# Embedding of patch tokens: four neighbours from five products instead of two from three

## The chip, the cores and the metric

One core of one Trainium2 chip runs the whole kernel. The metric is device time in microseconds (us), the median of three runs. Engines are called PE (TensorE, matmul), DVE (VectorE), ACT (ScalarE), POOL (GpSimd) and SP (SyncE, which here only issues transfers). SBUF is the working memory, 128 partitions wide; PSUM is where matmuls leave their results.

## What is computed

The reference cuts a signal into overlapping patches, takes a real Fourier transform of each, and embeds it with one matrix. What follows is one attention-like layer with a decaying memory and a mixture of eight experts, two of them for each token.

```python
# tokenizer: x is (4, 64, 512, 64) = (B, C, T, V); patches of 16 with stride 8, last value repeated 8 times
patches = xp[:, :, idx, :]                      # idx = n * 8 + 0..15, n = 0..63
xf = rfft(patches, axis=patch, norm='ortho')    # 9 frequencies
h = concat([xf.real, xf.imag]) @ W.T            # W is 256 x 1152: 16384 tokens of 256

# layer
z  = layernorm(layernorm(h))
q, k, v = z @ Wq.T + bq, z @ Wk.T + bk, z @ Wv.T + bv
mem[t] = decay * mem[t-1] + k[t] * v[t];  z1 = ln(h) + q * mem
h  = h + z1 + relu(layernorm(z1) @ W1.T + b1) @ W2.T + b2

# experts: the two best of eight for each token
tok = layernorm(h)
h  = h + tok + sum over the two experts e of weight_e * (gelu(tok @ w1[e] + b1[e]) @ w2[e] + b2[e])
```

Transform and W are linear, so they fold into one matrix over the 16 samples of a patch and the 64 channels. A patch is two halves of 8 samples, and neighbouring patches share a half. If s(n) is the n-th segment of 8 samples, token n is s(n) A + s(n+1) B, which is a short convolution along n.

## The kernel before

The tokens go through in 32 blocks of 512, four tiles of 128 each. A pair of samples shares a partition group, so a product with A or B is four matmuls of 128 x 128 by 128 x 256, summed in PSUM (J = 4). The folded weights are kept as E and O, the even and the odd frequencies, with A = E + O and B = E - O. Two neighbours come from three products: one of the odd segment with 2E, which both share, and one of each difference.

```python
weff = emb.tile([P, 2 * J, D], F32)          # E + O, E - O
wsum = emb.tile([P, J, D], F32)              # 2 E
xpool: bufs=2                                # xb, the segments of one block

def differences(self, xb):
    self.xd = emb.tile([P, 2, J, NV, NO], F32, name="xd")
    nc.vector.tensor_tensor(self.xd[:, 0], ev[:, :, :, :NO], od, ALU.subtract)     # L305
    nc.vector.tensor_tensor(self.xd[:, 1], ev[:, :, :, 1:], od, ALU.subtract)      # L306

def embed(self):
    ps = p_tm.tile([P, U, D], F32, name="tm")
    for u in range(U):                       # U = 2
        for j in range(J):
            nc.tensor.matmul(ps[:, u, :], lhsT=od[:, j, ts(u, P)], rhs=wsum[:, j, :], ...)   # L317
    ms = emb.tile([P, U, D], F32, name="ms")
    nc.scalar.copy(ms, ps)                   # L321
    for u in range(U):
        yield                                # other work of PE comes in between
        ps = p_tm.tile([P, 2, D], F32, name="tm")
        for i in range(2):
            for j in range(J):
                nc.tensor.matmul(ps[:, i, :], lhsT=xd[:, i, j, ts(u, P)], rhs=weff[:, i * J + j, :], ...)  # L328
        nc.vector.tensor_tensor(self.h[:, u::U, :], ps, ms[:, u:u+1, :].to_broadcast([P, 2, D]), ALU.add)  # L335
        for i in range(2):
            norm.stats(self.h, i * U + u)    # bn_stats, bn_aggr
    norm.factors(twice=True)                 # rstd, on GpSimd
    norm.apply(self.zz, self.h, 1)
    norm.apply(self.z, self.h, 0)
```

What follows in a block, with the buffers that matter. `zz` and `tok` are turned into features by a transposing DMA through 16-bit halves; `turned` has one buffer, and the join reads it.

```python
class Turn:
    def start(self, planes):                                     # L272
        self.turned = one.tile([P, TT, 2, KD, P], U16, name="turned")
        ... nc.sync.dma_start(out=turned part, in_=plane, transpose=True)
    def join(self, dst, copy):                                   # L278: hT and tokT
        ...

def retention(self, m):                                          # m = 0, 1
    pk = feature_mm(wqkv_sb[:, 1], self.hT, m)                   # L284, bank mm of four
    nc.scalar.activation(own_order(ks), tiles_order(pk), AF.Identity, bias=...)
    pv = feature_mm(wqkv_sb[:, 2], self.hT, m)
    nc.vector.scalar_tensor_tensor(kv, tiles_order(pv), bv, ks, ALU.add, ALU.mult)      # L374
    nc.vector.tensor_tensor_scan(ks, decay, kv, carry, ALU.mult, ALU.add)               # L382
    pq = feature_mm(wqkv_sb[:, 0], self.hT, m)
    nc.vector.scalar_tensor_tensor(tiles_order(ret), tiles_order(pq), bq, ks, ALU.add, ALU.mult)   # L392
```

The order of PE, DVE, ACT and SP is written by hand. One turn of the loop works on three blocks (`new`, `mid`, `old`); `slot` takes in one tile of expert work (`enter` L734, `leave` L751 and its DVE part L760 to L767, and the scatter-add `out<-y,xg` on GpSimd, L771) where there is one. At that point three banks of PSUM serve `tm`.

```python
for i in range(NS):                          # NS = 31
    embed = new.embed();  next(embed)
    mid.features2()                          # join of hT on ACT
    old.rows();  old.turn3()                 # tok of old into turned
    next(embed);  next(embed, None)
    slot(known)
    old.join3()                              # tokT, on DVE
    for m in range(8):
        mid.mlp_in(m)
        if m == 1: new.split1()              # zz of new into turned
        if m == 3: slot(known)
        if m == 5: new.features1()           # hT of new, on DVE
    old.logits(0..3)
    blocks[i + 1].differences(xs.pop(i + 1))
    new.retention(0);  old.choose();  new.retention(1)
    take(old.i + 1, old, old.place())        # place: L560 on PE, then 8 scatters xbuf<-row, L576, on GpSimd
    xs[i + 2] = load_x(i + 2)                # L90
    slot(known);  mid.mlp_out(0);  new.residual()      # zz<-z, h sums
    slot(known);  new.split2();  mid.mlp_out(1)        # tok<-h
```

## Time and profile before

| | |
|---|---|
| time, median of 3 runs | 2275.05 us (2271.82 to 2275.25) |
| span of the profiled run | 2277.5 us, mean TensorE clock 0.987 |
| matmul instructions of the embedding, L317 and L328 | 512 and 1024; 120.2 and 230.6 us busy |
| DVE differences, L305 and L306 | 32 each; 1213 and 1222 ns each |
| DVE additions L335 | 64; 672 ns each |
| DVE bn_stats and bn_aggr of h | 256 and (with those of z) 384; 411 and 182 ns each |
| DVE kv and ret, L374 and L392 | 64 each; 748 and 1112 ns each |
| one block in the middle, kv to kv | 65.7 us (1182.50 to 1248.20) |

A group's row in the profile gives the line, the engine, the output and the inputs by the program's names, the shape, the number of instructions, their total and mean time, and the idle time just before them with what ended it. One fp32 matmul of the program stands as two instructions in the trace. A view of waits lists who waited for whom. The chain that ended last is followed back from the last instruction, at each step to what released it. A timeline gives single instructions with start and duration; a bracket at its end is the engine's idle time before the instruction, with the releaser.

### The profile page before, as it was taken

Reading aid. Unit: us, or ns where it says so; the run is one execution under the profiler, and the core shown is the slowest. Engines: PE = TensorE matmul, PEld = TensorE weight load, DVE = VectorE, ACT = ScalarE, POOL = GpSimd, SP = SyncE. Lnnn points to the kernel's source line nnn. Section 1 sums busy time; section 2 is a strip of 40 time slices with the busy share of each in tenths; the row PEclk is TensorE's granted clock in tenths of the full one; section 3 lists DMA queues with packets and bytes.
Section 4 is the critical chain, followed back from the end, with each engine's and each line's share of the span. In section 5 each row is a group of like instructions: output and inputs, shape, how many; then the busy total and the mean of one; then the engine's idle time right before and its main releaser. Section 6 shows DMA issues by size and latency. Waiting matters only on the chain.

```text
span 2277.5 us, 28306 instructions
## 1 busy us (share of the span) xinstructions
PE 2191.8 (96%) x8652; PEld 1574.0 (69%) x8652; DVE 1490.3 (65%) x4427; ACT 784.9 (34%) x1213; POOL 863.2 (38%) x822
## 2 busy tenths in 40 slices
PE   3999999999999999999999999999999999997997
PEld 2666667777776677777667777676677777675775
DVE  6567666666666667666766666666667666757464
ACT  1222243333334333333343333334333333332332
POOL 0012224444443344443334444443444443335344
PEclk9999999999999999999999999999999999998999
DMA  5133357656656675566667656656665565595653
GB/s 150 28 94 82 102 128 158 136 128 135 143 129 131 150 158 118 130 140 138 136 131 159 132 130 134 143 128 132 152 152 123 131 140 137 117 180 111 120 68 46
DMA packets 461671, 289.14 MB, mean 127 GB/s; under 512 B 377936, under 2 KB 432336, under 8 KB 457424
## 3 DMA queue, kind: packets, MB, share of 16 engines
q1 hardware_dynamic: 410464, 214.44, 40.1%
q0 software_dynamic: 49632, 67.39, 16.9%
q10 hardware_dynamic: 1424, 5.52, 0.9%
q8 instruction: 68, 1.11, 0.2%
q14 instruction: 83, 0.68, 0.1%
HBM read 116.81 MB, written 88.39 MB: 90 GB/s over the span
## 4 chain that ended last, share of the span: by engine, by line
PE 51%; DVE 24%; POOL 11%; issue 7%; DMA 6%; ACT 0%; POOLq 0%; DVEq 0%; SPq 0%; ACTq 0%
PE mm L284 24%; PE tm L328 9%; POOL xbuf L576 8%; PE mm L734 5%; PE tm L751 5%; DMA out<-y,xg 4%; DVE ks L382 3%; DVE ret L392 3%; POOL out L771 2%; PE sm L493 2%; DVE kv L374 2%; DVE zz L238 2%; PE tm L442 2%; DVE h L417 1%; DVE h L416 1%
## 5 line engine op out<-in xcount | busy, mean ns | idle before, releaser
L771 POOL DMA_INDIRECT out<-y,xg x262 | 433.7, 1655 | 550.0 <-DVE y L767 302.4
L442 PE MATMUL tm<-w_sb,aT 128*128 128x256 f32 x2048 | 453.3, 379 | 1.7 <-DVE taken L671 1.1
L284 PE MATMUL mm<-hT,w_sb 128*128 128x512 f32 x1024 | 449.9, 593 | 1.6 <-ACT hT L278 1.1
L442 PEld LDWEIGHTS tm<-w_sb,aT 128*128 128x128 f32 x2048 | 388.6, 190 | 55.6 <-DVE taken L671 1.4
L284 PEld LDWEIGHTS mm<-hT,w_sb 128*128 128x128 f32 x1024 | 194.1, 190 | 223.0 <-issue 212.4
L284 PE MATMUL mm<-hT,wqkv_sb 128*128 128x512 f32 x768 | 342.9, 603 | 3.7 <-DVE hT L278 3.7
L576 POOL DMA_INDIRECT xbuf<-row,to x248 | 244.2, 985 | 257.2 <-DVE full L635 169.8
L742 ACT ACTIVATE ge<-mm,w 128x256 f32<-128x256 f32 x262 | 109.3, 469 | 522.0 <-issue 503.1
L284 PEld LDWEIGHTS mm<-hT,wqkv_sb 128*128 128x128 f32 x768 | 145.7, 193 | 175.8 <-issue 166.0
L734 PE MATMUL mm<-xT,w 128*128 128x256 f32 x1048 | 253.3, 385 | 9.7 <-DVE tile_share L760 9.1
L751 PE MATMUL tm<-w,ge 128*128 128x256 f32 x1048 | 248.8, 380 | 0.0
L434 ACT ACTIVATE aT<-mm,vec 128x512 f32<-128x512 f32 x256 | 171.3, 685 | 219.2 <-PE mm L284 218.2
L328 PE MATMUL tm<-weff,xd 128*128 128x256 f32 x1024 | 230.6, 384 | 16.8 <-DVE y L765 8.6
L328 PEld LDWEIGHTS tm<-weff,xd 128*128 128x128 f32 x1024 | 193.3, 191 | 53.2 <-DVE y L765 19.1
L734 PEld LDWEIGHTS mm<-xT,w 128*128 128x128 f32 x1048 | 196.2, 192 | 47.3 <-issue 23.2
L751 PEld LDWEIGHTS tm<-w,ge 128*128 128x128 f32 x1048 | 200.3, 191 | 31.1 <-issue 3.8
L727 ACT COPY xT<-xh 128x512 uint16<-128x512 uint16 x262 | 181.3, 761 | 39.7 <-DMA xh<-xbuf 32.4
L264 ACT COPY planes<-zz 128x1024 uint16<-128x1024 uint16 x122 | 121.5, 1043 | 206.0 <-DVE zz L238 206.0
L229 POOL TENSOR_SCALAR rstd<-mv 128x4 f32<-128x4 f32 x93 | 37.2, 400 | 328.2 <-DVE mv L210 326.1
L317 PE MATMUL tm<-wsum,xb 128*128 128x256 f32 x512 | 120.2, 389 | 25.8 <-ACT wsum L121 25.8
L238 DVE TENSOR_SCALAR zz<-z,mv,rstd 128x256 f32<-128x256 f32 x128 | 44.4, 410 | 137.7 <-POOL rstd L234 137.7
L533 POOL TENSOR_TENSOR ex<-euler,second 128x4 f32<-128x4 f32 x32 | 34.8, 1089 | 262.0 <-DVE second L525 262.0
(147 smaller groups left out, 2343.8 us busy)
## 6 DMA issues: line engine op xcount, KB each, us to landing
w<-in_wex SPq DMA_DIRECT2D x109, 641.5 KB
xb<-in_x SPq DMA_DIRECT2D x32, 1040.0 KB
out<-h SPq DMA_DIRECT2D x31, 512.0 KB
bank<-in_wex ACTq DMA_DIRECT2D x8, 641.5 KB
out<-y,xg POOLq DMA_INDIRECT x262
xbuf<-row,to POOLq DMA_INDIRECT x248
xh<-xbuf SPq DMA_TRANSPOSE x131
xg<-xbuf SPq DMA_DIRECT2D x131, 4.0 KB
```

Of the source, the lines that this page charges most:

```text
L264: nc.scalar.copy(planes[:, :, i * D : (i + 1) * D], half)
L284: nc.tensor.matmul(ps, lhsT=w[:, k, ts(m, P)], rhs=rhs[:, k, :], start=k == 0, stop=k == KD - 1)
L317: nc.tensor.matmul(ps[:, u, :], lhsT=od[:, j, ts(u, P)], rhs=wsum[:, j, :], start=j == 0, stop=j == J - 1)
L328: nc.tensor.matmul(ps[:, i, :], lhsT=xd[:, i, j, ts(u, P)], rhs=weff[:, i * J + j, :], start=j == 0, stop=j == J - 1,)
L434: nc.scalar.activation(self.aT[:, m, :], ps, AF.Relu, bias=vec[:, MB1 + m : MB1 + m + 1])
L442: nc.tensor.matmul(ps[:, i, :], lhsT=self.aT[:, k, ts(u * 2 + i, P)], rhs=w2_sb[:, k, :], start=k == 0, stop=k == KH - 1,)
L576: write = nc.gpsimd.indirect_dma_start(out=xbuf, out_offset=bass.IndirectOffsetOnAxis(ap=to[:, c, t : t + 1], axis=0), in_=self.row[:, t, ...
L727: nc.scalar.copy(halves[:, :, :, 1 - i], self.xh[:, i * KD : (i + 1) * KD, :])
L734: nc.tensor.matmul(ps[:, m, :], lhsT=self.w[:, k * D + m * P : k * D + (m + 1) * P], rhs=self.xT[:, k, :], start=k == 0, stop=k == KD - 1,)
L742: nc.scalar.activation(self.ge[:, m, :], ps[:, m, :], AF.Gelu, bias=self.w[:, 5 * D + m : 5 * D + m + 1])
L751: nc.tensor.matmul(ps[:, c, :], lhsT=self.ge[:, k, ts(c, P)], rhs=w[:, (2 + k) * D : (3 + k) * D], start=k == 0, stop=k == KD - 1,)
L771: add = nc.gpsimd.indirect_dma_start(out=out, out_offset=bass.IndirectOffsetOnAxis(ap=self.xg[:, c, NUMBER - D : NUMBER - D + 1], axis=0), ...
```

## The change

With segments in four classes by n mod 4, four neighbouring tokens are four outputs of the two-tap convolution. Toom-Cook's scheme evaluates at five points and gets them from five products instead of six (twice three): 5 x 4 = 20 matmuls for a block instead of 24. For it the kernel makes five linear combinations of the segments (nine DVE operations of 512 elements instead of two of 1024), five weight matrices (E, O, 3E - O, E + O, E - O), and recombines the products with factors of 1/6 to 4/3 (seven scalar_tensor_tensor of 256 and one addition, instead of two additions of 512). A tile now holds the tokens with the same n mod 4, so the orders of retention, of the stores and of the row numbers change from two interleaved tiles to four. To make room, `xb` has one buffer instead of two, and the first two steps change places: block 0's combinations come ahead of the load of block 1.

```diff
-    xpool = early.enter_context(tc.tile_pool(name="xp", bufs=2, side="right"))
+    xpool = early.enter_context(tc.tile_pool(name="xp", bufs=1, side="right"))
...
-    weff = emb.tile([P, 2 * J, D], F32)
-    wsum = emb.tile([P, J, D], F32)
+    wu = emb.tile([P, 5, J, D], F32)
...
-            if odd == 0:
-                nc.scalar.mul(wsum, eo[:, 0], 2.0)
-        nc.vector.tensor_tensor(weff[:, 0:J, :], eo[:, 0], eo[:, 1], ALU.add)
-        nc.vector.tensor_tensor(weff[:, J:, :], eo[:, 0], eo[:, 1], ALU.subtract)
+        nc.vector.scalar_tensor_tensor(wu[:, 3], wu[:, 1], 3.0, wu[:, 2], ALU.mult, ALU.subtract)
+        nc.vector.tensor_tensor(wu[:, 0], wu[:, 1], wu[:, 2], ALU.add)
+        nc.vector.tensor_tensor(wu[:, 4], wu[:, 1], wu[:, 2], ALU.subtract)
...
-        return out[ts(i, BLK), :].rearrange("(u q r) d -> q r u d", q=P, r=2)
+        return out[ts(i, BLK), :].rearrange("(q t) d -> q t d", q=P)
...
         def differences(self, xb):
-            self.xd = emb.tile([P, 2, J, NV, NO], F32, name="xd")
-            nc.vector.tensor_tensor(self.xd[:, 0], ev[:, :, :, :NO], od, ALU.subtract)
-            nc.vector.tensor_tensor(self.xd[:, 1], ev[:, :, :, 1:], od, ALU.subtract)
+            self.xv = emb.tile([P, 5, w, NQ], F32, name="xv")
+            v = [self.xv[:, i] for i in range(5)]
+            # more(to, a, by, b): to = a * by + b, scalar_tensor_tensor; less(to, a, b): to = a - b, tensor_tensor
+            less(v[1], s3, s2)
+            less(v[2], s2, s1)
+            more(v[2], v[2], -2.0, v[1])
+            more(v[1], s1, -2.0, v[1])
+            less(v[3], s3, s1)
+            less(v[0], s0[:, :, :NQ], s2)
+            more(v[0], v[0], 2.0, v[3])
+            less(v[4], s0[:, :, 1:], s2)
+            more(v[4], v[3], -2.0, v[4])
...
         def embed(self):
+            a, b = products((1, 2))
+            nc.scalar.copy(q, a)
+            scaled(p, b, 1.0 / 3, q, ALU.add)
+            scaled(q, b, -1.0 / 3, q, ALU.add)
+            yield
+            c, m0 = products((3, 0))
+            scaled(h[2], c, 2.0 / 3, p, ALU.subtract)
+            scaled(h[1], c, 1.0 / 3, q, ALU.subtract)
+            scaled(h[0], m0, 0.5, p, ALU.subtract)
+            scaled(h[0], c, 1.0 / 6, h[0], ALU.add)
+            scaled(h[3], c, 4.0 / 3, q, ALU.subtract)
+            for t in range(TT - 1):
+                norm.stats(self.h, t)
+            yield
+            m4, _ = products((4,))
+            nc.vector.tensor_tensor(h[3], m4, h[3], ALU.add)
+            norm.stats(self.h, TT - 1)
...
             def tiles_order(a):
-                return a.rearrange("p (r w) -> p w r", r=2)
+                return a.rearrange("p (r w) -> p w r", r=TT)
...
-        xs[1] = load_x(1)
         blocks[0].differences(xs.pop(0))
+        xs[1] = load_x(1)
```

(The removed body of `embed` is the one shown above; `scaled(to, a, by, b, op)` is a scalar_tensor_tensor with to = a * by op b; `products` makes four matmuls for each product into one bank `tm`.)

## The prediction

> **What bounds the kernel now.** I read the busy shares first, then who TensorE waits for, then the chain that ended last over one block, then VectorE's timeline of that block.

> The shares seem to settle it:

> ```profile
> PE 2191.8 (96%) x8652; PEld 1574.0 (69%) x8652; DVE 1490.3 (65%) x4427; ACT 784.9 (34%) x1213; POOL 863.2 (38%) x822
> ```

> TensorE (PE) is busy 96% of the span, VectorE (DVE) 65%. From 360 to 1971 us PE is busy 1602.7 of 1611 us at a full clock. The waits of PE (releaser; total us, times, longest us) are as small:

> ```profile
> PE tm L317 <- ACT wsum L121: 25.8, 1, 25.8
> PE mm L734 <- DVE tile_share L760: 9.1, 2, 7.7
> PE tm L328 <- DVE y L765: 8.6, 26, 0.7
> ```

> The first is the start-up. The third matters: in 26 blocks PE is stopped for 0.3 us by a VectorE result, so something is nearly as long as PE. The chain that ended last, 1180 to 1250 us (start, us, what), shows it:

> ```profile
> 1182.50 0.76 DVE kv L374
> ...
> 1195.04 1.06 POOL xbuf L576
> ...
> 1207.22 3.02 DMA out<-y,xg
> ...
> 1210.26 1.38 DVE zz L238 x4
> ...
> 1214.31 0.70 DVE y L765
> ...
> 1215.06 7.17 PE tm L328 x32
> ```

> From kv to y (1182.50 to 1215.02, 32.5 us) the path runs on VectorE and GpSimd; only then does PE take over, until the next kv at 1248.20. A block lasts 65.7 us. Now VectorE's timeline of that second half (the bracket is idle time before the instruction, and its releaser):

> ```profile
> 1220.65 1.38 DVE L238 TENSOR_SCALAR tok<-h,mv,rstd 128x256 f32<-128x256 f32 x4 [3.18 <-POOL rstd L234]
> ...
> 1223.21 0.68 DVE L335 TENSOR_TENSOR h<-tm,ms 128x512 f32<-128x512 f32 x1
> ...
> 1233.44 1.46 DVE L278 COPY tokT<-turned 128x512 uint16<-128x512 uint16 x4
> ...
> 1240.37 1.46 DVE L278 COPY hT<-turned 128x512 uint16<-128x512 uint16 x4 [2.99 <-DMA turned<-planes]
> 1241.73 1.21 DVE L305 TENSOR_TENSOR xd<-xb 128x1024 f32<-128x1024 f32 x1
> 1242.86 1.22 DVE L306 TENSOR_TENSOR xd<-xb 128x1024 f32<-128x1024 f32 x1
> 1248.20 0.75 DVE L374 SCALAR_TENSOR_TENSOR kv<-mm,vec,ks 128x512 f32<-128x512 f32 x1 [4.12 <-PE mm L284]
> ```

> Read upward from kv. It waits 4.12 us for PE, the only place on this loop where VectorE waits for PE. Before it stand the two differences, before them the join into hT, which waits for a transposing DMA. That DMA starts at 1234.96, just as the tokT join ends (1234.90): turned has one buffer, and the tokT join is its reader. The tokT join follows the embedding's additions and norm. So a **second loop** runs beside PE without needing it: kv, placing, GpSimd's scatters and rstd, zz, y, rstd, tok, embedding, norm, tokT join, DMA, hT join, differences, kv. Its length is the period less the wait at kv. Over blocks 8 to 30 that wait is 2.6 to 4.1 us, mean 3.73, so the second loop has 65.7 - 3.73 = **62.0 us**.

> [...]

> **The change, part by part** (steady block)

> *PE.* A matmul here is two instructions: L328's 16 matmuls stand as x32 in 7.17 us, so 0.448 us each. 24 become 20: -4 x 0.448 = **-1.79 us**, and PE needs 63.9 us. If PE alone counted, 32 blocks would give -57 us, 2218.

> *Differences.* Two operations of 1024 elements become nine of 512. Old: 1241.73 to 1244.08, 2.35 us. New durations: five subtractions at 0.69 us (the 512-element tensor_tensor), four multiply-adds at 0.75 (kv's form). An independent successor starts about 0.08 us before the end (L305 to L306: 1.13 us apart, 1.21 long); one that needs the result starts 0.03 later than the end (the small operations of choose: 0.19 long, 0.22 apart). Three subtractions (v2, v0, v4) feed the next operation: 3 x 0.72. Two subtractions do not: 2 x 0.61. Four multiply-adds: three at 0.67 and the last in full, 2.76. Sum 6.14. **+3.8 us**, all between the hT join and kv.

> *Recombination.* Old: two additions of 512 from PSUM and four bn_stats pairs, 1223.21 to 1226.87, 3.66 us. New: seven multiply-adds of 256 (L117's form, 0.48 long, 0.40 apart), one of them feeding its neighbour: 6 x 0.40 + 0.51 = 2.91; three statistics pairs at 0.55, 1.64; one addition of 256, about 0.45 with its dependence (0.69 less half of 0.53, plus 0.03); the last pair 0.64. Sum 5.64. **+2.0 us**, ahead of rstd, zz and the tokT join. The SyncE queue gives no cover: its last issue before the transposing DMA (xg at 1233.90, 0.41 long) ends 0.6 us before the tokT join.

> *ACT.* The copy ms of 512 becomes 256; off the path.

> *DMA.* xb has one buffer instead of two, so its load can only go out after the eighth difference operation, 5 to 6 us later than the old 1243.07. It has until the next block's differences, over 50 us: hidden. The store of h has one run of 4 KB per partition instead of two of 2 KB; nobody waits for it.

> *Steady sum.* Second loop: 62.0 + 3.8 + 2.0 = 67.8 us against PE's 63.9. The period becomes the longer one: 67.8 - 65.7 = **+2.1 us** in place of -1.8. PE then idles 3.9 us in each block. Blocks 7 to 30, 24 periods: **+50 us**.

> *Start.* PE began at 25.8 us with eight matmuls that needed only half the prepared weights. Now both halves are needed, plus three combinations (0.1 to 0.3 us over the old two, and 1.2 more for the third) and nine differences. Old statistics of block 0 ended at 49.8 us. New: preparation to 36.7, the first difference 0.6, three weight combinations 3.5, the other eight differences 5.5 us, so v ends near 46.5; PE's second pair of products near 51; combination and statistics near 56. About +6, then +3.8 for the differences of block 1 ahead of block 0's kv less its 1.97 wait: **+7**.

> *Early blocks.* Blocks 1 and 2 still wait for PE in VectorE (7.9 us at L335, 5.3 at L449), so they gain back little and lose little: +2. The kv waits of blocks 3 to 6 are 1.01, 2.72, 2.49 and 4.02 us; 4 x 5.8 - 10.2 = 13, of which block 5 hides some (its hT waits 9.1 us for the DMA). **+13** with blocks 1 and 2.

> *Tail.* From 2030 us the load of the expert bank and PE's remaining work set the end: 0 to +2.

> Sum: 2275 + 50 + 7 + 13 + 1 = **2346 us**.

> **Rivals.**
> 1. PE stays the bound: 2218 to 2230 us. For it: 96% busy, hardly a wait. Against: the slack of the other loop is 3.73 us, the addition 5.8 us, and the removal of 1.79 us from PE shortens only PE's loop. It would need VectorE's operations at a third of their measured cost.
> 2. The recombination's 2.0 us is hidden (the DMA of turned is held by the SyncE queue after all, or runs shorter), and only the differences count: 62.0 + 3.8 = 65.8 us, the same period as now; with the start, about 2290. For it: the queue ends only 0.0 to 0.6 us ahead of the tokT join.
> 3. A new wait: the single xb buffer. If the load landed late, differences would wait in each block. Against: over 50 us for 1 MB at a mean of 127 GB/s (8 us alone). I give it little.
> 4. Strides of four make ret or kv dearer: each 0.1 us twice a block is 6 us in all. [...]

> **Range and chances.** The largest uncertainty is the sum of sixteen added operation times less the slack: 0.8 us of error in it is 24 x 0.8 = 20 us, and rival 2 pulls low. 80%: 2300 to 2372 us. The limit for slower by 2% is 2320.6 us: 0.80. Same: 0.15, mostly rival 2. Faster: 0.05, rival 1.

> **What would show it.** In the profile after: PE busy below 92% though the matmul count of the embedding falls from 768 to 640; a block period of 67 to 68.5 us; the kv of retention no longer waiting for PE; new waits of PE for hT before retention and for `both` at the placing matmuls, together 3 to 4 us in each block; the nine difference operations at 6.1 us and tok to last statistics 2 us longer. It is wrong if kv still waits for PE (then the second loop was shorter than I read), or if the join into tokT moves while the transposing DMA's start doesn't (rival 2), or if xd's successor xv waits for xb (rival 3).

## The result, and the profile after

The changed kernel takes **2351.1 us** (median of 4 runs, 2345.1 to 2351.6) against 2273.4 us for the one before (4 runs): a ratio of 1.0336, 95% interval 1.0316 to 1.0356. It is 3.4% slower though it does a sixth less matrix work in the embedding (the L333 groups hold 1280 matmul instructions, 1536 before). One slow execution of a_bank_late below, 4102.4 us at a granted clock of 0.745, is left out of its median.

The busy shares of the changed kernel, the first line of its page:

```profile
PE 2173.1 (92%) x8396; PEld 1534.7 (65%) x8396; DVE 1649.7 (70%) x4844; ACT 777.4 (33%) x1212; POOL 856.7 (36%) x822
```

PE has fallen from 96% to 92% and VectorE gone from 65% to 70%. No engine is full any more: each now waits in a circle for others. The waits of PE (what waited, for whom; total us, times, longest us) name one such circle:

```profile
PE tm L333 <- DVE xv L307: 43.2, 1, 43.2
PE tm L770 <- ACT row L488: 31.9, 16, 2.2
PE tm L770 <- DVE pq L339: 19.8, 10, 2.0
PE tm L333 <- DVE y L784: 14.2, 26, 1.1
...
PE sm L579 <- DVE both L550: 6.8, 5, 1.8
```

The first line is the start-up. The second and third are the same wait, 26 times at 2.0 us: L770 is an expert's second product, and it wants a bank of PSUM. The row copy on ScalarE named in 16 of the 26 ends at the same instant as VectorE's pq (1329.75 and 1329.74 us in one block) and does not touch that bank; pq does, and in all 26 L770 starts 0.15 us after the end of pq. `both`, where the prediction looked for a wait in every block, stops PE 5 times.

VectorE's timeline of one block, 1190 to 1221 us (start, duration, instruction; in brackets the idle time before it and its releaser):

```profile
1191.68 1.38 DVE L234 TENSOR_SCALAR tok<-h,mv,rstd 128x256 f32<-128x256 f32 x4 [3.16 <-POOL rstd L230]
...
1194.24 0.88 DVE L339 SCALAR_TENSOR_TENSOR pq<-tm,pq 128x256 f32<-128x256 f32 x2
...
1206.06 1.46 DVE L274 COPY tokT<-turned 128x512 uint16<-128x512 uint16 x4
...
1213.05 1.46 DVE L274 COPY hT<-turned 128x512 uint16<-128x512 uint16 x4 [3.94 <-DMA turned<-planes]
1214.40 1.28 DVE L310 TENSOR_TENSOR xv<-xb 128x512 f32<-128x512 f32 x2
...
1220.31 0.74 DVE L395 SCALAR_TENSOR_TENSOR kv<-mm,vec,ks 128x512 f32<-128x512 f32 x1
```

kv, which waited 4.12 us for PE before, has no bracket here: VectorE is late, not PE. The nine combinations take 1214.40 to 1220.31, 5.91 us. But look at the top as well: p and q, the first readers of the embedding's first bank, stand behind tok and the h + tok addition, which wait 3.16 us for GpSimd's rstd. PE's own timeline at that place:

```profile
1195.26 1.96 PE L770 MATMUL tm<-w,ge 128*128 128x256 f32 x8 [1.97 <-DVE pq L339]
1197.06 7.03 PE L280 MATMUL mm<-hT,w_sb 128*128 128x512 f32 x16
```

The three `tm` banks go in turn: products 1 and 2, products 3 and 0, product 4, then the expert's product, which gets the first bank again. In the kernel before, ScalarE emptied that bank (`ms`). Now ScalarE copies one half and VectorE reads the other, twice, in its own order. So PE stands still until VectorE has come by.

One block later the same stop has a second effect. VectorE and PE, 1255 to 1292 us:

```profile
1262.04 2.79 PE L770 MATMUL tm<-w,ge 128*128 128x256 f32 x8 [2.02 <-DVE pq L339]
1264.63 7.94 PE L280 MATMUL mm<-hT,w_sb 128*128 128x512 f32 x16
...
1288.22 0.75 DVE L395 SCALAR_TENSOR_TENSOR kv<-mm,vec,ks 128x512 f32<-128x512 f32 x1 [0.93 <-PE mm L280]
```

The same eight instructions take 2.79 us where they took 1.96, the next sixteen 7.94 where they took 7.03, and kv waits for PE again. The table by stretches of 3.41 us (busy us of PE, PEld, DVE, ACT, POOL with counts; then granted clock, DMA share, GB/s) shows why:

```profile
1191.34:1194.76 3.42, 1.95 (x10) 1.37 (x8) 3.01 (x7) 3.25 (x5) 0.42 (x2) 1.00 0.24 34
...
1259.62:1263.03 3.41, 1.40 (x7) 0.92 (x7) 3.31 (x8) 3.41 (x6) 0.00 (x0) 1.00 0.33 129
1263.03:1266.44 3.41, 3.41 (x8) 2.02 (x7) 3.07 (x11) 2.93 (x6) 0.08 (x1) 0.50 0.26 64
```

After the stop the granted clock is 0.50 for 3.41 us in the second case and stays at 1.00 in the first. The stretches are not chosen freely. The starts of the 12 drops in the 24 steady blocks, at 454.07, 590.61, 792.00 us and so on, lie whole multiples of 3.413 us apart, so they stand on one grid. The stop ahead of 1262.04 lies within one step of this grid (PE busy 1.40 of 3.41 us); the one ahead of 1195.26 is divided between two steps. So it is in all 24 blocks: the 12 stops that lie within one step are followed by a drop, and the 12 that a step's end divides are not. Exactly the blocks with a drop have periods of 67.8 to 68.06 us; the other twelve have 66.5 to 67.2, but for one of 68.75. Before, the period was 65.73.

So there are two loops, both longer than PE's work:

- **The second loop** of the prediction: 62.0 us before, plus 3.56 (combinations, 5.91 for 2.35) plus 1.6 (tok to last statistics, 5.2 for 3.66) makes 67.1. That is, within some 0.2 us, the period of the blocks without a clock drop.
- **The held bank**, which the prediction did not have: from kv to the end of pq VectorE and GpSimd need 41.7 us (1220.31 to 1262.04); from there PE needs 24.4 us to the end of the product that kv reads, at full clock. That is 66.1 us, just under the second loop; with the clock drop it is 41.7 + 26.2 = 67.9, just over it. The combinations are not in this loop.

### The profile page after: what moved, and what is told of

Its sections match the earlier page's. It is cut to its first block, busy times and chain, and to the rows that moved or that the text cites. A ratio compares the mean times of both kernels' runs of the same rounds, so it can differ in the third digit from the quotient of the medians.

```text
span 2349.8 us, 28175 instructions
## 1 busy us (share of the span) xinstructions
PE 2173.1 (92%) x8396; PEld 1534.7 (65%) x8396; DVE 1649.7 (70%) x4844; ACT 777.4 (33%) x1212; POOL 856.7 (36%) x822
## 3 DMA queue, kind: packets, MB, share of 16 engines
q0 software_dynamic: 49632, 67.39, 16.4%
## 4 chain that ended last, share of the span: by engine, by line
PE 49%; DVE 25%; DMA 9%; POOL 8%; issue 5%; ACT 2%; SPq 1%; POOLq 0%; DVEq 0%; ACTq 0%
PE mm L280 21%; PE tm L770 7%; PE tm L463 6%; PE mm L753 6%; PE tm L333 5%; POOL xbuf L595 4%; DMA turned<-planes 3%; DMA out<-y,xg 3%; POOL out L790 2%; DVE ks L403 2%; DVE zz L234 2%; DVE st L205 2%; DVE ret L413 2%; PE sm L512 1%; DVE xv L310 1%
## 5 line engine op out<-in xcount | busy, mean ns | idle before, releaser
L790 POOL DMA_INDIRECT out<-y,xg x262 | 428.3, 1635 | 558.8 <-DVE y L786 297.9
L280 PE MATMUL mm<-hT,w_sb 128*128 128x512 f32 x1024 | 466.5, 609 | 7.3 <-ACT hT L274 4.7
L280 PEld LDWEIGHTS mm<-hT,w_sb 128*128 128x128 f32 x1024 | 201.6, 198 | 241.5 <-issue 215.6
L333 PE MATMUL tm<-wu,xv 128*128 128x256 f32 x1280 | 293.1, 385 | 57.4 <-DVE xv L307 43.2
L333 PEld LDWEIGHTS tm<-wu,xv 128*128 128x128 f32 x1280 | 243.9, 192 | 100.7 <-DVE xv L307 43.2
L770 PE MATMUL tm<-w,ge 128*128 128x256 f32 x1048 | 259.3, 392 | 51.7 <-ACT row L488 31.9
L770 PEld LDWEIGHTS tm<-w,ge 128*128 128x128 f32 x1048 | 201.6, 194 | 92.1 <-ACT row L488 37.8
L234 DVE TENSOR_SCALAR zz<-z,mv,rstd 128x256 f32<-128x256 f32 x128 | 44.4, 410 | 141.3 <-POOL rstd L230 141.2
L274 DVE COPY hT<-turned 128x512 uint16<-128x512 uint16 x124 | 45.5, 449 | 135.3 <-DMA turned<-planes 135.3
```

The source lines that it names most:

```text
L234: nc.vector.tensor_scalar(dst[:, t, :D], src[:, t, :], self.mv[:, t, 0:1], self.rstd[:, i, t : t + 1], ALU.subtract, ALU.mult,)
L280: nc.tensor.matmul(ps, lhsT=w[:, k, ts(m, P)], rhs=rhs[:, k, :], start=k == 0, stop=k == KD - 1)
L333: nc.tensor.matmul(ps[:, n, :], lhsT=xv[:, i, j, :], rhs=wu[:, i, j, :], start=j == 0, stop=j == J - 1)
L770: nc.tensor.matmul(ps[:, c, :], lhsT=self.ge[:, k, ts(c, P)], rhs=w[:, (2 + k) * D : (3 + k) * D], start=k == 0, stop=k == KD - 1,)
L790: add = nc.gpsimd.indirect_dma_start(out=out, out_offset=bass.IndirectOffsetOnAxis(ap=self.xg[:, c, NUMBER - D : NUMBER - D + 1], axis=0), ...
```

## The experiments

The theory was the prediction's second loop; its rival at first that total VectorE work counts whatever its place. After reading the trace above a second rival came up: the held bank. In the lists below the times are medians, and each ratio is to the kernel before, with its 95% interval; "period" is the mean of the 24 steady blocks in the profile, kv to kv. Kernels with "cheap" in the name leave the embedding's proper values out: they have the time of the structure, not its result.

**b_diff2 and b_diff3: is there slack in the kernel before, and how much?** In the kernel before, the two differences run twice or three times.

```diff
+            for _ in range(2):        # b_diff3: 3
                 nc.vector.tensor_tensor(self.xd[:, 0], ev[:, :, :, :NO], od, ALU.subtract)
                 nc.vector.tensor_tensor(self.xd[:, 1], ev[:, :, :, 1:], od, ALU.subtract)
```

> The kernel before with its two differences done twice: 2.35 us more of VectorE between the hT join and kv in each block, nothing else. Second-loop theory: the kv wait of 3.7 us takes it in, the steady period stays at 65.7 us and kv then waits about 1.4 us; only the early blocks, with kv waits of 1.0 to 2.7 us, lose a little: 2275 to 2283 us. Rival, VectorE's total work counts because it is nearly as long as PE's: 32 x 2.35 = +75 us, 2350.

> The kernel before with its differences done three times: 4.70 us more between the hT join and kv. Second-loop theory: 4.70 less the kv wait of 3.73 is +1.0 us for each steady block, period 66.7 us, 24 x 1.0 = 24 us, and 8 to 12 us in the start and the early blocks: 2300 to 2315 us; kv no longer waits for PE. Rival of total work: +150 us. Rival that PE alone is the bound: 2275.

Measured: 2282.4 us, 1.0021 (1.0010 to 1.0032), period 65.87, kv still waiting about 1.7 us; and 2305.3 us, 1.0120 (1.0093 to 1.0147), period 66.40, kv never waiting. The first repeat is nearly free, the second is not: the slack is 3.7 to 4 us, as read from the wait at kv, and VectorE work as such does not count until it is used up.

**a_diff_cheap: are the combinations the cost?** In the changed kernel, from block 1 on, two subtractions of 1024 elements stand for the nine combinations (v4 stays block 0's; the embedding is left out).

```diff
-            less(v[1], s3, s2) ... more(v[4], v[3], -2.0, v[4])          # nine
+            nc.vector.tensor_tensor(flat[:, :half], xb[:, :half], xb[:, half:2*half], ALU.subtract)
+            nc.vector.tensor_tensor(flat[:, half:2*half], xb[:, half:2*half], xb[:, :half], ALU.subtract)
```

> The changed kernel with the nine combinations of each block after the first replaced by two subtractions of 1024 elements (the products are then not those of the embedding). Theory of the prediction, the second loop alone: 67.5 less 3.6 is PE's own 63.9 us, total about 2235. Rival from the trace after: the bank of products 1 and 2 is freed only when VectorE comes to p and q behind tok, and PE's expert product waits 2.0 us for it. That loop (kv to p and q 41.7 us, then PE to the next kv 24.4 us) doesn't contain the differences: the period stays at 66.1 us, or 67.8 where the clock drops behind the stop: 2290 to 2330.

Measured: 2330.9 us, 1.0218 (1.0179 to 1.0257), against some 2235 if the second loop were all. Its periods are a mix of 66.2 and 67.9, kv waits 2.9 or 4.6 us for PE, and its waits of PE still hold the same entry:

```profile
PE tm L777 <- ACT row L495: 35.1, 18, 2.2
PE tm L777 <- DVE pq L346: 13.9, 7, 2.0
```

With 3.6 us taken off the second loop the block hardly gets shorter, and the two periods are those of the held-bank loop, 66.1 and 67.9. The second loop alone is refuted: two loops of nearly one length, and shortening one is worth little.

**a_rec_cheap: are the recombination and the bank the cost?** ScalarE copies the first bank whole, and two additions of 512 stand for the eight operations (the recombination is left out; the nine combinations stay).

```diff
-            nc.scalar.copy(q, a);  scaled(p, b, ...);  scaled(q, b, ...)
+            nc.scalar.copy(pq, ps)
...
-            scaled(h[2], c, ...) ... tensor_tensor(h[3], m4, h[3], ALU.add)
+            nc.vector.tensor_tensor(self.h[:, 0:2, :], ps, pq, ALU.add)
+            nc.vector.tensor_tensor(self.h[:, 2:4, :], ps[:, 0:1, :].to_broadcast([P, 2, D]), pq, ALU.add)
```

> The changed kernel with the seven scaled additions of 256 and one of 256 replaced by two additions of 512, and the bank of products 1 and 2 copied out whole by ScalarE as in the kernel before (the embedding is not computed). The nine combinations stay. If the bank held for p and q and the 1.5 to 2.0 us of recombination are real: no wait of PE at the expert product, no clock drop, period 62.0 + 3.6 = 65.6 us, total about 2285. If the differences alone made the loss, the time stays near 2345.

Measured: 2273.5 us, 0.9986 (0.9974 to 0.9999), period 65.32. Freeing the bank by ScalarE and shortening the recombination brings back 78 us, more than expected. It changes both loops at once, so it cannot divide the cost between them. The next one takes only p and q (0.9 us) off the second loop.

**a_pq_early: the held bank freed, all work kept.** Products 1 and 2 of the next block, p and q are issued one step earlier, in VectorE's wait for rstd ahead of tok.

```diff
-                mid.mlp_out(1)
+                mid.mlp_out(1, lambda: embeds.update({i + 1: start(i + 1)}))   # called between norm.factors and norm.apply
...
-            embed = new.embed();  next(embed)
+            embed = embeds.pop(i) if i in embeds else start(i)
```

> The changed kernel with one move: the products 1 and 2, their copy and p and q come ahead of tok in VectorE's order, into its 3.2 us wait for rstd, so the bank is free when PE comes to the expert product. All work is kept. Held-bank theory: no 2.0 us stop of PE there, no clock drop, and 0.9 us less between tok and the statistics: period 67.5 to about 66.0, total 2351 - 24 x 1.5 - some 10 in the tail = 2300 to 2310. If the held bank were only a place where PE waits for a loop that is as long elsewhere, the period falls by the 0.9 us alone: about 2330.

Measured: 2298.9 us, 1.0087 (1.0055 to 1.0119), period 66.12. The 2.0 us wait at the expert product is gone, and the granted clock is 1.00 from 407 to 1994 us (0.99 over the same blocks of the changed kernel). `both`, which the prediction had named, now stops PE 29 times; hT does so only 6 times. After the start-up line, the waits of PE are:

```profile
PE sm L583 <- DVE both L554: 39.3, 29, 1.8
PE tm L333 <- DVE y L788: 20.4, 26, 1.1
```

The remaining period fits the second loop less the 0.9 us of p and q, which have left it: 67.1 - 0.9 = 66.2. Of the 52 us gained the steady blocks give 24 x 1.37 = 33, block 31 another 14 (96.4 for 110.6).

**a_diff_move: combinations into VectorE's waits.** Seven go into the wait ahead of zz, two into the one ahead of tok.

```diff
-            blocks[i + 1].differences(xs.pop(i + 1))
+            combine = blocks[i + 1].combinations(xs.pop(i + 1))
...
-            new.residual()
+            new.residual(lambda: next(combine))          # seven, between factors and apply
-                mid.mlp_out(1)
+                mid.mlp_out(1, lambda: next(combine, None))   # two
```

> The changed kernel with the nine combinations moved out of the stretch between hT and kv: seven into VectorE's 5.1 us wait for rstd ahead of zz, two into the 3.2 us wait ahead of tok; the load of xb follows them. All work is kept. Held-bank theory: as with the cheap combinations, period 66.1 us or 67.9 where the clock drops, kv waits 3 to 4.7 us for PE: 2320 to 2340. Theory of the second loop alone: about 2245.

Measured: 2375.7 us, 1.0433 (1.0397 to 1.0469), period 68.29, a miss by over 35 us. kv now waits 3.7 to 6.9 us for PE: the second loop did get shorter. But zz came later (kv to y 33.35 us for 32.5), and zz is part of the held-bank loop, which got longer. The work was moved from the loop that had a rival to the one that became the longest.

**a_both_move: both moves.**

```diff
+ a_pq_early's edit and a_diff_move's edit together
```

> Both moves together, all work kept. The loop without PE is then 62.0 - 2.35 + 1.55 - 0.9 = 60.3 us, below PE's 63.9; if PE is then the bound, 24 x 1.8 us come off the time before, the start keeps its 8 us: 2225 to 2240, faster than the kernel before by some 2%. [...]

Measured: 2288.2 us, 1.0053 (1.0036 to 1.0070), period 65.47, mostly 65.14 where 63.9 was hoped for. The path from kv to y became 33.3 us, 32.5 before. GpSimd's timeline from 1280 to 1300 us shows where:

```profile
1288.21 0.51 POOL L225 TENSOR_SCALAR rstd<-mv 128x4 f32<-128x4 f32 x1
1288.80 1.46 POOL L230 TENSOR_TENSOR rstd<-rstd,mhalf 128x4 f32<-128x4 f32 x1
...
1299.87 1.04 POOL L230 TENSOR_TENSOR rstd<-rstd,mhalf 128x4 f32<-128x4 f32 x1
```

The two small operations of rstd ahead of zz take 0.51 and 1.46 us beside VectorE's combinations (one runs from 1288.66 for 0.69 us); in the kernel before and in the changed one they take 0.23 and 1.04 us at this place. These 0.7 us are most of the 0.8 by which the path to y grew; the rest of the way from 63.9 to 65.14 us was not traced. Over the 93 instructions of each kind in the run they average 507 and 1399 ns; 400 and 1256 in the kernel before, 402 and 1256 in the changed one. So this wait for GpSimd was not free to be filled with the combinations: it became longer by 0.7 us.

**a_both_cheap: what is the saving on PE worth?** The edits of a_diff_cheap and a_rec_cheap together (the embedding is left out); VectorE then has the work of the kernel before, PE the twenty matmuls.

```diff
+ a_diff_cheap's edit and a_rec_cheap's edit together
```

> The changed kernel with both cheap parts: two subtractions in place of nine combinations and two additions of 512 in place of the recombination (the embedding is not computed); what is left of the change is 20 matmuls for 24 and the preparation. PE is then the bound at 63.9 us: 2225 to 2240. If the matmuls' saving were worth nothing, 2275.

Measured: 2234.0 us, 0.9819 (0.9783 to 0.9856), period 64.13, kv waiting about 2.2 us for PE. PE is all but the bound (it still waits 0.3 us a block for y, as in the kernel before), and four matmuls fewer are worth 65.73 - 64.13 = 1.6 us a block. That is the saving which the change aimed at, without its price.

**a_split: all work kept, put where neither loop has it.** a_pq_early, and five of the nine combinations ahead of the hT join, in VectorE's wait for the transposing DMA (3.94 us above); four stay behind it.

```diff
                 if m == 5:
+                    combine = blocks[i + 1].combinations(xs.pop(i + 1))
+                    next(combine)                        # five
                     new.features1()
...
-            blocks[i + 1].differences(xs.pop(i + 1))
+            next(combine, None)                          # four
...
+ a_pq_early's edit
```

> The changed kernel, all work kept, with p and q ahead of tok and the nine combinations split: five ahead of the hT join, in its 3.9 us wait for the transposing DMA, four (2.6 us) where all nine stood. Nothing is added ahead of zz. Loop without PE: 62.0 + 0.3 + 1.55 - 0.9 = 63.0 us; loop over y and the second products: 32.5 + 33.05 - 1.79 = 63.8 us; PE 63.9 us. Period about 64.0 us, total 2230 to 2245, some 1.5% faster than the kernel before. If the move of the combinations was what cost the 1.2 us over PE's time in the kernel with both moves (beside rstd on GpSimd), it is gone here; if the cost is in the loop elsewhere, the period stays above 65 us, 2270 to 2290.

Measured: **2233.1 us, 0.9820 (0.9795 to 0.9844)**, period 64.02. Its first line, and VectorE's timeline from 1270 to 1300 us:

```profile
PE 2136.3 (96%) x8396; PEld 1522.9 (68%) x8396; DVE 1650.0 (74%) x4844; ACT 771.0 (35%) x1212; POOL 856.9 (38%) x822
```

```profile
1286.13 1.28 DVE L314 TENSOR_TENSOR xv<-xb 128x512 f32<-128x512 f32 x2
...
1290.23 1.47 DVE L274 COPY hT<-turned 128x512 uint16<-128x512 uint16 x4 [0.76 <-DMA turned<-planes]
...
1295.44 0.75 DVE L400 SCALAR_TENSOR_TENSOR kv<-mm,vec,ks 128x512 f32<-128x512 f32 x1 [1.12 <-PE mm L280]
```

VectorE has the same 4844 instructions and 1650 us of work as in the changed kernel; only the order differs. The wait for the DMA has shrunk to 0.76 us because work fills it, and kv waits 1.12 us for PE again, so the second loop no longer binds. PE is busy 96%; in 26 blocks it still waits some 0.3 us for y, as in the kernel before. It beats both kernels: 118 us under the changed one, 42 under the kernel before (2274.9 us when measured with it).

**a_split_sums and b_sums: one more move, and a fair comparison.** The sums of h with z and the bias (2.4 us, behind zz) move to the wait ahead of tok; once on top of a_split, once in the kernel before.

```diff
         def residual(self):
-            self.h += z;  self.h += mb2                  # two tensor_tensor of 1024
+        def sums(self): ...                              # called in mlp_out(1), between factors and apply
```

> As the split version, and the two additions into h of 1024 elements (2.4 us) behind zz move into the wait ahead of tok, so that y is done 2.4 us earlier and PE doesn't wait for the bank of the expert's product at the second products. If that loop (63.8 us) still holds PE at times, the period falls to 63.6 to 63.9 us, 2225 to 2240; the wait ahead of tok is then overfull by 0.1 us, which the loop without PE has room for.

> The kernel before with the same move of the two additions into h: the 0.3 us stop of PE at the second products goes, in 26 blocks: 2265 to 2272 us, period 65.4 us. It says what the move is worth without the change.

Measured: 2236.3 us, 0.9809 (0.9789 to 0.9829), the same as a_split, and 2258.6 us, 0.9919 (0.9900 to 0.9938), better than expected. In the kernel before the move takes away PE's wait for y, period 65.15. On top of a_split it does so too, and 16 of the 24 steady blocks of the profiled run (2246.4 us, the longest of six) take 63.40 to 63.82 us. But seven of the other eight have a clock drop and take up to 67.4, so the mean is 64.32, and the last block takes 97.1 us for 89.7. Six of these drops follow a stop of 0.35 to 0.86 us ahead of retention; just before each of these stops PE ran 16 matmuls of only 8 columns for 1.85 us. So a_split was not yet at PE's own time, which is 63.4 us; the kernel before had 16 us left in its own order, and the Toom-Cook scheme in its best order is 25 us ahead of that, not 42.

**a_bank_late: the tail.** In the changed kernel's last step, the loads of the expert bank go out only once the last hT join is on its way.

```diff
-            if m in (1, 2, 4, 5, 7):
-                next(weights)
...
+            if m >= KH - 3:
+                next(weights)
...
```

> The changed kernel with one difference in the tail: the loads of the expert bank (8 of 0.64 MB) start after the join of hT of the last block instead of at the second step of the MLP, so the transposing DMA of that block doesn't stand behind them. In the changed kernel this join waits 21.9 us (13.0 before) and the last block is 12 us longer than before. If the collision of the two is the cause, the wait falls to 4 to 6 us and 8 to 15 us come off the 2351, less what is lost where the bank then arrives later: 2337 to 2345. If the tail is bound by the bank's own 5.1 MB, no gain: 2350 or more.

Measured: 2331.0 us (2330.5 to 2340.4), 1.0274 (1.0247 to 1.0301), some 20 us less than the changed kernel and below the range expected. The steady period stays at 67.39; block 31 takes 92.8 us for 110.6. The timeline of the tail, 2060 to 2160 us, first of the changed kernel, then of this one:

```profile
2080.48 0.33 ACTq L702 DMA_DIRECT2D bank<-in_wex  x1
...
2084.78 9.03 SPq L268 DMA_TRANSPOSE turned<-planes  x1
...
2108.23 1.46 DVE L274 COPY hT<-turned 128x512 uint16<-128x512 uint16 x4 [21.92 <-DMA turned<-planes]
```

```profile
2083.53 3.32 SPq L268 DMA_TRANSPOSE turned<-planes  x1
2087.03 0.38 ACTq L702 DMA_DIRECT2D bank<-in_wex  x1
2089.44 1.47 DVE L274 COPY hT<-turned 128x512 uint16<-128x512 uint16 x4 [4.38 <-DMA turned<-planes]
```

Beside the bank loads the issue of one transposing DMA takes 9.03 us, and its data come 23 us after the issue began; ahead of them 3.32 and 6 us. The collision was there before (hT waited 13.0 us in the tail); the change moved the transpose further into it.

## Why the prediction came out right, and where it was wrong

The total was 2346 us for a measured 2351.1, but its terms missed in both directions. In the profiled spans (2349.8 less 2277.5, 72.3 us):

| step | predicted | measured | how read |
|---|---|---|---|
| start | +7 | +9.0 | kv of block 0 at 68.14, 59.13 before |
| early blocks | +13 | +8.2 | kv of block 6 17.2 us later, less 9.0 |
| steady, 24 blocks | +50 | +42.2 | 67.49 for 65.73 |
| tail | +1 | +12.8 | block 31 110.56 for 98.72; +1.0 behind it |

**The second loop: right in kind and size.** It was read as 62.0 us; b_diff2 and b_diff3 show its slack, a_pq_early shows it alone. Combinations came to 5.91 us for 6.14, the recombination to 5.2 for 5.64: the spacing of the 256-element operations was mis-sized, p and q ending 0.88 us after the first began. These make 67.1 us instead of 67.8, that is 17 us less over 24 blocks.

**"A block period of 67 to 68.5 us" held, for a partly other reason.** The step that failed is the list of what could bind: it asked what the added operations lengthen, not what they hold. p and q were counted at 0.80 us in the second loop; that they also replace ScalarE as the reader that frees a PSUM bank was not looked at, and rival 4 looked for a further cost in strides only. The held bank gives PE's 2.0 us stop at L770. The waits predicted "for hT before retention and for `both`" are mostly not there; the one for `both` appears in a_pq_early, once the bank is free. "PE busy below 92%" was just missed: 2173.1 of 2349.8 us is 92.5%.

**The granted clock was left out of the sum.** The prediction has no term for it; here a stop of 2.0 us was followed by a clock of 0.50 in 12 of 24 steady blocks. It adds about 0.8 us to each of these blocks (67.9 for 67.1), some 10 of the 42.2 us. The sum agrees: 24 x (67.1 - 65.73) = 33, and 10. Nor does every stop of this length count alike: 1.96 us within one step of the 3.413 us grid was followed by a drop, 1.94 us in another step was not.

**PE's own time was read too long.** The 63.9 us start from a period of 65.7 in which PE still waited for y; without that wait most blocks take 65.13 us in b_sums and, with the four matmuls fewer, 63.40 in a_split_sums.

**"The kv of retention no longer waiting for PE" is half right:** in the 12 blocks with the drop it waits 0.74 to 1.02 us.

**The tail was mis-sized**, +1 for +12.8: "the load of the expert bank and PE's remaining work set the end" named both, but not that the last transposing DMA meets the bank loads, and that a delay shifts it further among them. a_bank_late takes back some 20 us, of which 17.8 in block 31. The tail depends on more than this change: with more work in each block, b_diff2 takes 92.2 us for block 31 where the kernel before takes 98.7 (one profile each).

**Rivals.** Rival 1 (PE stays the bound) is what a_both_cheap and a_split are, 2234 and 2233 us, slightly above the 2218 to 2230 given; the change as written is not it. Rival 2 did not occur: the tokT join and the DMA behind it moved together. Rival 3 did not occur: the load of xb starts at 1219.70 and lands 4.8 us later, and nothing waits for it. Of rival 4, ret kept its 1.10 us with tiles by n mod 4 (1.11 before).

**What stays open.** Why six clock drops of a_split_sums follow stops of only 0.35 to 0.86 us, each stop behind 1.85 us of matmuls of 8 columns; block 8's 68.75 us; and the start and the early blocks, which were read from the trace and not undone by an experiment. a_split with the late bank loads was not run.

## What to carry to other kernels

An added operation has two costs: the time it adds to the loops it lies on, and the buffer it keeps while it stands behind the work ahead of it (p and q behind tok: PE stopped for 2.0 us a block); so for each new reader ask what it releases, and behind what it stands. A loop's slack can be read in one block as the wait at the place where it joins the bound engine; here 2.35 us, below a slack of 3.7 to 4 us, added 0.14 us to the period (b_diff2), and 4.70 us, beyond it, 0.67 (b_diff3). When two loops have nearly one length, shortening one alone gains little, and only a change to both shows what was to be gained: here 3.6 us off the second loop gained 0.5 us a block (a_diff_cheap), and with the bank freed and the recombination shortened as well 3.4 us (a_both_cheap).
